# Softmax transposed through DRAM in the first and third attention, and the NF4 comparisons moved to GpSimd

## The chip, the core and the metric

The program runs on one core of one Trainium2 chip. A core has TensorE for matrix products, which writes to PSUM; VectorE, ScalarE and GpSimd for work on vectors; and queues on which transfers between DRAM and the on-chip memory (SBUF) are issued, here nearly all on the queue of SyncE (SP), some of the last stage's on ScalarE's. Each engine works through its own instructions in order and waits for the others at semaphores. The metric is the time of the device for one execution, in microseconds (us).

## The reference

An activation x of 8 batches x 128 tokens x 512 features passes through four blocks; each adds an attention and then a feed-forward layer to x, both on a layernorm of x. All is float32 unless said. In the order of the work:

- first attention: cross-attention to a context of 128 tokens per batch, 32 heads of 128, RMS norm of the queries' input, position bias, mask, softmax, output projection added to its normalised input;
- first feed-forward: a base matrix plus eight low-rank experts, weighted by a sparsemax;
- second attention: 8 small heads over windows of the features; second feed-forward: 8-bit integer weights;
- third attention: 32 query heads on 8 key heads, rotary embedding, mask, softmax;
- third feed-forward: gate, up and down matrices of 1376 x 512, which are first rounded to NF4: each block of 64 weights is divided by its largest magnitude, each quotient replaced by the nearest of 16 code values, and multiplied by the magnitude again;
- fourth attention with RMS norms on queries and keys, and a fourth feed-forward with 64 routed low-rank parts.

What the change touches is computed as:

```python
score = jax.nn.softmax(score, axis=-1)
attn = jnp.einsum('bhqk,bkhd->bqhd', score, h_v)
...
idx = jnp.searchsorted(bounds, normalized)
return (NF4_CODE[idx] * absmax).reshape(shape)
```

## The kernel before

x stays in SBUF. The batches are taken in two halves of four (128 tokens each, so 512 columns).

**The loop of units.** First and third attention are cut into units: one half, one head. A group is four heads, and there are 8 groups per half: 64 units of the first attention (`Unit0`), then 64 of the third (`Unit2`). The loop over `units` is a pipeline. In the turn of unit u, TensorE is given: the transposes of u's softmax (`turn`), the projections of unit u+3 (`pieces`; in the first attention keys and queries, in the third queries, and for head 0 also keys and values), the scores of unit u+2 (`score`), the product of u's softmax with the values (`weigh`), and the work after it (`after`). `after` is, in the first attention, behind head 3 of a group, four times a value projection for the next group and an output projection; in the third attention, two output projections of the previous group behind heads 0 and 1 each. So the scores of a unit are computed two turns before its softmax is used.

`score` evicts the scores from PSUM with VectorE (adding bias or mask), and `softmax` takes the row maximum (VectorE), the exponentials (ScalarE, four instructions) and the reciprocal of the sum; the scaling by it is VectorE's in the first attention and ScalarE's in the third. The result lies with queries on the partitions; the product with the values needs keys there. `turn` calls `p_transposed`: four transposes on TensorE into PSUM (L225), and a copy to SBUF by ScalarE (L228).

In the third attention the rotary embedding of a projection is three VectorE products out of PSUM (L640, L642, L643) and an add on GpSimd (L644).

**Work in between.** Between these pieces the loop calls `slot()`. It does what `short_stages` has put into a table: the first feed-forward, the second attention and the second feed-forward of one half of the batches run while the units of the other half go on. And at a pace per stage (`NF4_PACE`) it advances `nf4_items`, the rounding of the third feed-forward's weights, by steps.

**NF4 rounding.** The code value is built as a sum over 15 thresholds: each adds its step where the quotient is beyond it. In `nf4_round` the first threshold writes `dq` (L708); each of the other 14 is a VectorE TENSOR_SCALAR that compares with the threshold and multiplies by the step into `ind` (L712), and a VectorE add of `ind` to `dq` (L713). There are 34 such chunks, mostly of 128x512, 476 pairs in all. The results are transposed and stored to DRAM (`d1` to `d3`).

**The last stages.** The third feed-forward and the fourth attention follow the loop. The fourth attention's transposes already take a way through DRAM (`L3.far`): VectorE transposes blocks of 32x32 (`V.transpose`, L948), a store writes the tile to DRAM, and four loads read it back with the blocks in their new places.

**What sets the order.** The tile framework that the kernel is written in orders each engine's instructions, DMA issues included, by its own estimate of times, and adds the semaphores. An engine's program may therefore depart from the order of the source: of TensorE's pieces as of SP's issues. Tiles of one tag share a fixed number of buffers, and a tile waits for one to come free: weights go through a ring of 20 tiles of 256 KB (`wpool`, tag `w`), scores through three (`score_tile`, tag `s`, which the fourth attention's `o` shares), transposed softmaxes through two (`pt`).

Of the kernel before, what the change touches and what calls it, by code (L numbers as in the profile page):

```python
# [11 lines left out]
F32 = mybir.dt.float32  # L12
F16 = mybir.dt.float16
BF16 = mybir.dt.bfloat16
# [4 lines left out]
ALU = mybir.AluOpType  # L19
# [4 lines left out]
P = 128  # L24
# [4 lines left out]
HALF = 4  # L29
# [15 lines left out]
NF4_STEPS = []  # L45
# [17 lines left out]
def kernel(ctx: ExitStack, tc: tile.TileContext, a, out):  # L63
    nc = tc.nc
    V, S, G, T = nc.vector, nc.scalar, nc.gpsimd, nc.tensor

    def pool(name, bufs, **kw):
        return ctx.enter_context(tc.tile_pool(name=name, bufs=bufs, **kw))
# [9 lines left out]
    ap_ = pool("att", 2)  # L78
    dram = pool("scratch", 1, space=DRAM)

    class Stream:


        def __init__(self, name, sb, ps, banks):
            self.name, self.sb, self.ps, self.banks = name, sb, ps, banks
# [26 lines left out]
    def load(dst, src):  # L112
        nc.sync.dma_start(dst, src)
# [26 lines left out]
    def batches(hf):  # L140
        return range(hf * HALF, (hf + 1) * HALF)
# [51 lines left out]
    def xt_tile():  # L193
        return xtp.tile([P, DC, 512], F32, tag="xT", name="xT")
# [26 lines left out]
    def p_transposed(st, p, engine=None):  # L221

        tp = st.tp()
        for h in range(4):
            T.transpose(tp[:, h, :], p[:, h, :], ident)  # L225
        pt = st.wide("pt", (P, 4, P))
        if engine is S:
            S.copy(pt, tp)  # L228
        else:
            V.tensor_copy(pt, tp)  # L230
        return pt
# [8 lines left out]
    def tile_of(name, bufs, shape=(P, 512)):  # L240
        return qkv.tile(list(shape), F32, tag=name, name=name, bufs=bufs)
# [2 lines left out]

    class Unit:
        def __init__(self, st, hf, g, h, group):
            self.st, self.hf, self.g, self.h, self.group = st, hf, g, h, group

        def softmax(self, s):
            st = self.st
            nm = st.small(4, "nm")
            V.tensor_reduce(nm, s, AX.X, ALU.max, negate=True)  # L254
            su = st.small(4, "su")
            exps(lambda i: s[:, i, :], lambda i: s[:, i, :], su, 4, nm)
            V.reciprocal(su, su)
            self.p, self.su = s, su
# [5 lines left out]
            return sc  # L264

        def score_tile(self):
            return ap_.tile([P, HALF, P], F32, tag="s", name="s", bufs=3)

        def turn(self):
            self.pt = p_transposed(self.st, self.p, S)  # L270

        def weigh(self):
            pv = self.st.pv()
            for i in range(HALF):
                T.matmul(pv[:, i, :], lhsT=self.values(i), rhs=self.pt[:, i, :], start=True, stop=True)  # L275
            o = tile_of("o", 6, (P, HALF, P))
            S.copy(o, pv)  # L277
            self.group.o.append(o)
# [424 lines left out]

    def nf4_round(dst, w):

        for i, (cmp, bound, step) in enumerate(NF4_STEPS):
            if i == 0:
                V.tensor_scalar(dst, w, bound, step, cmp, ALU.mult)  # L708
                continue
            ind = nfp.tile([P, 512], F32, tag="ind", name="ind", bufs=1)  # L710
            iv = ind[:w.shape[0], :w.shape[1]]
            V.tensor_scalar(iv, w, bound, step, cmp, ALU.mult)  # L712
            V.tensor_add(dst, dst, iv)  # L713
            yield

    def nf4_scales(ri, am):
# [5 lines left out]
    class Rows:  # L722
# [8 lines left out]
        def work(self):  # L731
            n, w = self.n, self.w
            wb = w.rearrange("p (k e) -> p k e", e=64)[:n]
            am = nfp.tile([P, 8], F32, tag="am", name="am")
            V.tensor_reduce(am[:n], wb, AX.X, ALU.max, apply_absolute_value=True)
            ri = nfp.tile([P, 8], F32, tag="ri", name="ri")
            nf4_scales(ri[:n], am[:n])
            yield
            V.tensor_tensor(wb, wb, along(ri[:n], 64), ALU.mult)
            yield  # L740
            dq = nfp.tile([P, 512], F32, tag="dq", name="dq", bufs=1)
            yield from nf4_round(dq[:n], w[:n])
            V.tensor_tensor(wb, dq.rearrange("p (k e) -> p k e", e=64)[:n], along(am[:n], 64), ALU.mult)
            yield
# [41 lines left out]
    class Pairs:  # L786
# [15 lines left out]
        def work(self):  # L802
            w, nw = self.w, self.nw
            self.scale(w, w, pair["rir"])
            yield
            dq = nfp.tile([P, 512], F32, tag="dq", name="dq", bufs=1)
            yield from nf4_round(dq[:, :2 * nw], w[:, :2 * nw])
            self.scale(w, dq, pair["amr"])
            yield
# [77 lines left out]
    class L3:  # L887
# [115 lines left out]
        def weigh(self, it):  # L1003
            pv = self.st.pv()
            for j in range(2):
                T.matmul(pv, lhsT=it.v[:, j, :], rhs=it.pts[j], start=j == 0, stop=j == 1)  # L1006
            it.o = ap_.tile([P, 4, P], F32, tag="s", name="o", bufs=3)
            if it.blocks:
                S.copy(it.o.rearrange("p h (a j) -> p a h j", j=32), pv.rearrange("p a (h j) -> p a h j", j=32))
            else:  # L1010
                S.copy(it.o, pv)
# [68 lines left out]
    with ExitStack() as early:  # L1080
        def sub_pool(name, bufs, **kw):
            return early.enter_context(tc.tile_pool(name=name, bufs=bufs, **kw))
# [3 lines left out]
        nfp = sub_pool("nf4", 2)  # L1086
# [18 lines left out]
        def slot():  # L1105
            for f, args in table.pop(now[0], []):
                f(*args)
            now[0] += 1
            due[0] += 0.0 if turning[0] else NF4_PACE[stage[0]][0 if table else 1]
            with tc.issue_after(mark[0].ins):  # L1110
                while due[0] >= 1.0:
                    due[0] -= 1.0
                    next(items, None)
# [3 lines left out]
        def drain():  # L1117
            while table:
                slot()

        def norm_pieces(i, box, b, get):

            def norm():
                box[b] = layernorm(side, b)

            def turn():
                S.copy(get()[:, :, cols(b)], transposed(side, box[b]))

            put(i, norm)
            put(i + 1, turn)  # L1130

        def l0_half(hf):
            box = {}

            def query(b):
                box[b] = l0_query(side, b)

            now[0] = 0
            for i, b in enumerate(batches(hf)):
                put(4 * i, l0_ctx, side, b)  # L1140
                put(4 * i + 1, query, b)
                put(4 * i + 3, lambda b: l0_turn(side, b, box[b]), b)
# [59 lines left out]
        units = []  # L1202
        for kind in (Unit0, Unit2):
            for hf in range(2):
                for g in range(NG):
                    grp = Group()
                    grp.v = []
                    units += [kind(main, hf, g, h, grp) for h in range(4)]

        xT0 += [xt_tile(), xt_tile()]  # L1210

        V.memset(xT0[1][:, 0, :], 0.0)
# [30 lines left out]
        for u, unit in enumerate(units):  # L1243
            stage[0] = u // (4 * NG)
            turning[0] = 8 * NG - 4 <= u < 8 * NG
            if u == 3:
                l0_half(1)
            if u in (4 * NG - 3, 8 * NG - 3, 12 * NG - 3):
                drain()
            unit.turn()  # L1250
            if u + 3 < len(units):
                for f in units[u + 3].pieces():
                    f()
                    slot()
            if u + 2 < len(units):
                units[u + 2].score()
            unit.weigh()
            if isinstance(unit, Unit2):
                slot()
            unit.after(units, u)  # L1260
            if u in (4 * NG - 1, 8 * NG - 1):
                short_stages((u + 1) // (4 * NG) - 1)
            if u == 12 * NG + 1:
                now[0] = 0
                xT.append(xt_tile())
                for b in batches(0):
                    norm_pieces(2 * b, {}, b, lambda: xT[0])
# [66 lines left out]
    n = len(items)  # L1334
# [96 lines left out]
def build(arrays):  # L1431
    import concourse.bacc as bacc

    nc = bacc.Bacc("TRN2", target_bir_lowering=False, num_devices=1)
    aps = {
        n: nc.dram_tensor(f"in_{n}", v.shape, mybir.dt.from_np(v.dtype), kind="ExternalInput").ap()
        for n, v in arrays.items()
    }
    out = nc.dram_tensor("out_0", (B, P, D), F32, kind="ExternalOutput").ap()
    with tile.TileContext(nc) as tc:  # L1440
        kernel(tc, aps, out)
    return nc
# [9 lines left out]
```

## Time and profile before

The median of three runs is 3138.36 us (3136.59 to 3139.01). The profile is of one execution:

| | |
|---|---|
| time of the profiled execution | 3138.55 us |
| its span, first to last instruction | 3136.8 us |
| mean granted TensorE clock | 0.999 of full speed |
| TensorE busy | 3119.5 us, 99% |
| VectorE busy | 1949.3 us, 62% |
| ScalarE busy | 1154.6 us, 37% |
| GpSimd busy | 292.0 us, 9% |
| first attention's units | about 30 to 1100 us |
| third attention's units | about 1100 to 1900 us |

How the profile is read: a group's row names the source line, the engine, the operation, output<-input tiles, shapes and the count, then the time that the group was busy, the mean of one instruction in ns, the idle time of the engine just before the group's instructions, and what ended it. A timeline's row has the start in us, the duration, the engine, the line, the operation with its tiles and the count of instructions merged into it; in brackets the idle time before it and what ended it. PE is TensorE, DVE VectorE, ACT ScalarE, POOL GpSimd; SPq are the issues on SP's queue, whose duration is that of issuing, not of the transfer. A matmul's recorded duration runs over the start of the next, as matmuls are pipelined; the distance between two starts says what one costs. A line can be that of a helper which several stages use: L225 and L228 also serve the second attention, L218 and L237 several projections.

### The profile page before, as it was taken

Reading aid. Unit: us, or ns where it says so; the run is one execution under the profiler, and the core shown is the slowest. Engines: PE = TensorE matmul, PEld = TensorE weight load, DVE = VectorE, ACT = ScalarE, POOL = GpSimd, SP = SyncE. Lnnn points to the kernel's source line nnn. Section 1 sums busy time; section 2 is a strip of 40 time slices with the busy share of each in tenths; the row PEclk is TensorE's granted clock in tenths of the full one; section 3 lists DMA queues with packets and bytes.
Section 4 is the critical chain, followed back from the end, with each engine's and each line's share of the span. In section 5 each row is a group of like instructions: output and inputs, shape, how many; then the busy total and the mean of one; then the engine's idle time right before and its main releaser. Section 6 shows DMA issues by size and latency. Waiting matters only on the chain.

```text
span 3136.8 us, 34834 instructions
## 1 busy us (share of the span) xinstructions
PE 3119.5 (99%) x11480; PEld 1744.5 (56%) x11480; DVE 1949.3 (62%) x4084; ACT 1154.6 (37%) x3535; POOL 292.0 (9%) x315
## 2 busy tenths in 40 slices
PE   9999999999999999999999999999999999999999
PEld 4555555545555555555556565445666656555554
DVE  5777777656667666887988873122654555555544
ACT  3322333235553233756343343001443434343332
POOL 2000000100001011111111110000111111111110
PEclk9999999999999999999999999999999999999999
DMA  6223222222223321112222212222556555555540
GB/s 210 87 71 91 90 91 80 74 70 75 74 66 89 115 85 55 56 55 71 82 87 73 76 59 59 76 61 93 184 173 183 180 179 174 178 177 164 179 132 14
DMA packets 324802, 328.24 MB, mean 105 GB/s; under 512 B 27600, under 2 KB 238736, under 8 KB 324112
## 3 DMA queue, kind: packets, MB, share of 16 engines
q1 hardware_dynamic: 301200, 283.03, 29.5%
q10 hardware_dynamic: 23040, 41.95, 4.3%
q8 instruction: 92, 1.51, 0.2%
q0 software_dynamic: 384, 1.05, 0.1%
q14 instruction: 86, 0.70, 0.1%
HBM read 259.15 MB, written 66.78 MB: 104 GB/s over the span
## 4 chain that ended last, share of the span: by engine, by line
PE 94%; DVE 4%; DMA 1%; ACT 1%; issue 0%; POOL 0%; SPq 0%; ACTq 0%; POOLq 0%; DVEq 0%
PE mm L237 20%; PE mm L218 14%; PE po L218 7%; PE tp L908 7%; PE mm L363 7%; PE mm L931 7%; PE mm L866 5%; PE pv L1006 4%; PE sc L983 3%; PE sc L263 3%; PE pv L275 3%; PE tp L225 3%; PE mm L875 2%; PE mm L653 2%; PE mm L663 1%; PE sc L519 1%
## 5 line engine op out<-in xcount | busy, mean ns | idle before, releaser
L237 PE MATMUL mm<-xT,w 128*128 128x512 f32 x1024 | 464.1, 595 | 0.2 <-DVE rot L643 0.2
L218 PE MATMUL mm<-w,o 128*128 128x512 f32 x1024 | 460.0, 594 | 0.0
L713 DVE TENSOR_TENSOR dq<-dq,ind 128x512 f32<-128x512 f32 (+2 forms) x476 | 326.2, 685 | 10.5
L218 PEld LDWEIGHTS mm<-w,o 128*128 128x128 f32 x1024 | 188.8, 190 | 217.0 <-issue 207.9
L237 PEld LDWEIGHTS mm<-xT,w 128*128 128x128 f32 x1024 | 188.7, 191 | 208.8 <-issue 202.8
L213 ACT ACTIVATE s<-s,nm 128x128 f32<-128x128 f32 x512 | 199.0, 390 | 149.1 <-DVE nm L254 144.0
L931 PE MATMUL mm<-w,xT 128*128 128x512 f32 x512 | 233.9, 592 | 0.0
L218 PE MATMUL po<-w,o 128*128 128x512 f32 x512 | 233.2, 594 | 0.0
L237 PE MATMUL mm<-ctxT,w 128*128 128x512 f32 x512 | 230.5, 593 | 1.8 <-ACT k L330 1.0
L363 PE MATMUL mm<-w,ctxT 128*128 128x512 f32 x512 | 230.4, 593 | 0.0
L712 DVE TENSOR_SCALAR ind<-nw 128x512 f32<-128x512 f32 (+2 forms) x476 | 218.6, 459 | 5.9
L213 ACT ACTIVATE p<-sc,nm,rq 128x256 f32<-128x256 f32 x256 | 141.1, 562 | 112.3 <-DVE nm L988 108.7
L219 DVE TENSOR_TENSOR x<-x,mm 128x512 f32<-128x512 f32 x128 | 87.5, 684 | 141.3 <-PE mm L218 140.9
L218 PEld LDWEIGHTS po<-w,o 128*128 128x128 f32 x512 | 96.3, 190 | 110.6 <-issue 103.3
L263 PEld LDWEIGHTS sc<-k,q 128*128 128x128 f32 x1024 | 131.0, 191 | 46.0 <-issue 44.4
L159 POOL TENSOR_TENSOR rs<-rs,mhalf 128x1 f32<-128x1 f32 x64 | 39.9, 625 | 1247.5 <-DVE rs L180 743.0
L363 PEld LDWEIGHTS mm<-w,ctxT 128*128 128x128 f32 x512 | 94.3, 190 | 106.2 <-issue 106.2
L866 PE MATMUL mm<-xT,w 128*128 128x512 f32 (+1 forms) x352 | 152.5, 592 | 0.8 <-DVE x L219 0.8
L277 ACT COPY o<-pv 128x512 f32<-128x512 f32 x128 | 74.4, 581 | 204.0 <-PE pv L275 203.9
L987 DVE TENSOR_REDUCE nm<-sc 128x2 f32<-128x512 f32 x128 | 85.3, 674 | 102.3 <-PE sc L983 102.0
L228 ACT COPY pt<-tp 128x512 f32<-128x512 f32 x192 | 108.9, 586 | 107.4 <-PE tp L225 107.3
L931 PEld LDWEIGHTS mm<-w,xT 128*128 128x128 f32 x512 | 97.0, 190 | 89.5 <-issue 84.7
(243 smaller groups left out, 4816.6 us busy)
## 6 DMA issues: line engine op xcount, KB each, us to landing
w<-in_l_wq SPq DMA_DIRECT2D x128, 256.0 KB
w<-in_l_wo SPq DMA_DIRECT2D x128, 256.0 KB
far<-tb SPq DMA_DIRECT2D x60, 512.0 KB
pt<-far SPq DMA_DIRECT2D x240, 128.0 KB
far<-tb SPq DMA_DIRECT2D x63, 384.0 KB
pt<-far SPq DMA_DIRECT2D x252, 96.0 KB
w<-in_l_wk SPq DMA_DIRECT2D x64, 256.0 KB
w<-in_l_wv SPq DMA_DIRECT2D x64, 256.0 KB
```

The costliest lines, as they stand in the source:

```text
L213: S.activation(dst(h), src(h), AF.Exp, bias=negm[:, h:h + 1], scale=by, accum_out=su[:, h:h + 1])
L218: T.matmul(mm, lhsT=o(h), rhs=wo[h], start=h == 0, stop=h == 3)
L228: S.copy(pt, tp)
L237: T.matmul(mm, lhsT=w[:, c, :], rhs=xT[:, c, :], start=c == 0, stop=c == DC - 1)
L263: T.matmul(sc[:, i, :], lhsT=self.q[:, i * P:(i + 1) * P], rhs=k[:, i * P:(i + 1) * P], start=True, stop=True)
L363: T.matmul(mm, lhsT=ctxT[:, c, toks(self.hf * HALF + i)], rhs=grp.wv[c], start=c == 0, stop=c == DC - 1)
L712: V.tensor_scalar(iv, w, bound, step, cmp, ALU.mult)
L713: V.tensor_add(dst, dst, iv)
L866: T.matmul(mm[:n, :], lhsT=w[c][:, j * P:j * P + n], rhs=xT[:, c, :], start=c == 0, stop=c == DC - 1)
L908: T.matmul(it.kv[:, s, :], lhsT=lhsT, rhs=it.wkv[c // 2][:, c % 2, :], start=c == 0, stop=c == DC - 1)
L931: T.matmul(mq, lhsT=self.xT[it.hf][:, c, cols(it.b)], rhs=it.wq[c], start=c == 0, stop=c == DC - 1)
L1006: T.matmul(pv, lhsT=it.v[:, j, :], rhs=it.pts[j], start=j == 0, stop=j == 1)
```

## The change

Two things change. First, all units of the first and third attention but the first three of the loop no longer transpose the softmax on TensorE. A new `turn_far`, called right after the unit's `score`, two turns before the unit is weighed, transposes 32x32 blocks on VectorE into a tile `tb` (one buffer), stores it to DRAM (256 KB), and loads it back into `pt` with four loads of 64 KB. `weigh` takes its operands as slices of that tile. Second, `nf4_round` lets GpSimd compare, writing zeros and ones as bfloat16 into `ind` (now two buffers, since the pool's default holds), one threshold ahead of the sum; VectorE multiplies by the step and adds in one SCALAR_TENSOR_TENSOR. The score tile's tag loses its third buffer and has the pool's default of two.

```diff
     class Unit:
         def __init__(self, st, hf, g, h, group):
             self.st, self.hf, self.g, self.h, self.group = st, hf, g, h, group
+            self.far = True
...
         def score_tile(self):
-            return ap_.tile([P, HALF, P], F32, tag="s", name="s", bufs=3)
+            return ap_.tile([P, HALF, P], F32, tag="s", name="s")

         def turn(self):
-            self.pt = p_transposed(self.st, self.p, S)
+            pt = p_transposed(self.st, self.p, S)
+            self.pt = [pt[:, i, :] for i in range(HALF)]
+
+        def turn_far(self):
+            tb = tile_of("tb", 1, (P, 4, HALF, 32))
+            V.transpose(tb, self.p.rearrange("p i (c k) -> p c i k", k=32))
+            far = dram.tile([4, 32, 4, P], F32, tag="far0", name="far0", bufs=4)
+            load(far.rearrange("a k b n -> (a k) (b n)"), tb.rearrange("p c i j -> p (c i j)"))
+            pt = self.st.wide("pt", (P, 4, HALF, 32))
+            for b in range(4):
+                load(pt[32 * b:32 * b + 32].rearrange("p a i j -> p a (i j)"), far[:, :, b, :].rearrange("a k n -> k a n"))
+            self.pt = [pt[:, :, i, :] for i in range(HALF)]

         def weigh(self):
             pv = self.st.pv()
             for i in range(HALF):
-                T.matmul(pv[:, i, :], lhsT=self.values(i), rhs=self.pt[:, i, :], start=True, stop=True)
+                T.matmul(pv[:, i, :], lhsT=self.values(i), rhs=self.pt[i], start=True, stop=True)
...
     def nf4_round(dst, w):
-        for i, (cmp, bound, step) in enumerate(NF4_STEPS):
-            if i == 0:
-                V.tensor_scalar(dst, w, bound, step, cmp, ALU.mult)
-                continue
-            ind = nfp.tile([P, 512], F32, tag="ind", name="ind", bufs=1)
-            iv = ind[:w.shape[0], :w.shape[1]]
-            V.tensor_scalar(iv, w, bound, step, cmp, ALU.mult)
-            V.tensor_add(dst, dst, iv)
+        def above(i):
+            cmp, bound, _ = NF4_STEPS[i]
+            ind = nfp.tile([P, 512], BF16, tag="ind", name="ind")[:w.shape[0], :w.shape[1]]
+            G.tensor_scalar(ind, w, bound, None, cmp)
+            return ind
+
+        then = above(1)
+        cmp, bound, step = NF4_STEPS[0]
+        V.tensor_scalar(dst, w, bound, step, cmp, ALU.mult)
+        for i in range(1, len(NF4_STEPS)):
+            ind = then
+            if i + 1 < len(NF4_STEPS):
+                then = above(i + 1)
+            V.scalar_tensor_tensor(dst, ind, NF4_STEPS[i][2], dst, ALU.mult, ALU.add)
             yield
...
+        for unit in units[:3]:
+            unit.far = False
...
-            unit.turn()
+            if not unit.far:
+                unit.turn()
...
             if u + 2 < len(units):
                 units[u + 2].score()
+                if units[u + 2].far:
+                    units[u + 2].turn_far()
             unit.weigh()
```

(The fourth attention's `o` loses `bufs=3` in the same way.)

More of the change, by code (lines that the diff above doesn't have):

```diff
@@ L1006, in weigh @@
                 T.matmul(pv, lhsT=it.v[:, j, :], rhs=it.pts[j], start=j == 0, stop=j == 1)
-            it.o = ap_.tile([P, 4, P], F32, tag="s", name="o", bufs=3)
+            it.o = ap_.tile([P, 4, P], F32, tag="s", name="o")
             if it.blocks:
```

## The prediction

> **What bounds the kernel now.** I read the page's busy times first, then who keeps TensorE waiting, then the timeline of the first and third attention, where the change works.
>
> ```profile
> span 3136.8 us, 34834 instructions
> PE 3119.5 (99%) x11480; PEld 1744.5 (56%) x11480; DVE 1949.3 (62%) x4084; ACT 1154.6 (37%) x3535; POOL 292.0 (9%) x315
> L225 PE MATMUL tp<-ident,s 128*128 128x128 f32 x768 | 112.2, 274 | 1.2 <-DVE s L521 0.6 <-ACT s L681 0.4
> ```
>
> TensorE is busy for 3119.5 of 3136.8 us, and its transposes of the softmax (L225) waited 1.2 us in all. In the waits of TensorE between 120 and 1890 us, which hold both attentions, no entry is above 0.9 us. So the time is the sum of TensorE's work, and every other engine runs inside it. "Busy" could hide slack, so the price of an instruction comes from the distance between starts (third attention, TensorE's timeline):
>
> ```profile
> 1668.87 1.06 PE L275 MATMUL pv<-pt,v 128*128 128x128 f32 x8
> 1669.76 0.60 PE L225 MATMUL tp<-ident,s 128*128 128x128 f32 x4
> 1670.20 3.60 PE L237 MATMUL mm<-xT,w 128*128 128x512 f32 x8
> 1673.63 1.05 PE L263 MATMUL sc<-k,q 128*128 128x128 f32 x8
> 1674.53 1.06 PE L275 MATMUL pv<-pt,v 128*128 128x128 f32 x8
> ```
>
> Four transposes hold TensorE for 1670.20 - 1669.76 = 0.44 us (not 0.60, the last drains under the next matmul), a projection for 3.43, scores 0.89, weighing 0.89. The granted clock is full throughout, so no change of clock is in the sum.
>
> **The change part by part.**
>
> Removed from TensorE: 128 units less the first 3, each 0.43 to 0.44 us: 125 x 0.43 = 54 us. Nothing else gets shorter on the engine that sets the end. From the profiled execution, whose time is 3138.55 us (span 3136.8 and 1.75 around it), that leaves 3084.6; from the median of 3138.36 it leaves 3084.4. This is the floor.
>
> Removed from ScalarE: 125 copies at 586 ns (L228), 73 us. It waited for TensorE anyway, so nothing for the end.
>
> VectorE: each of 476 thresholds loses its TENSOR_SCALAR and keeps one two-input instruction.
>
> ```profile
> L713 DVE TENSOR_TENSOR dq<-dq,ind 128x512 f32<-128x512 f32 (+2 forms) x476 | 326.2, 685 | 10.5
> L712 DVE TENSOR_SCALAR ind<-nw 128x512 f32<-128x512 f32 (+2 forms) x476 | 218.6, 459 | 5.9
> ```
>
> The new step-and-sum should cost what L713 does (the SCALAR_TENSOR_TENSOR of L678 takes 688 ns at 128x512): 219 us go. It gains 125 block transposes of 128x512. The rows are 960 ns for 128x768 and 1238 for 128x1024 (L948), 1.09 ns per element, so about 0.68 us each, 85 us. Without blocking, VectorE does 134 us less.
>
> GpSimd: 476 comparisons, a form that the trace does not have. Bounds: TENSOR_TENSOR of 128x128 takes 458 ns and of 128x512 1268 (fixed part 188 ns); the one operation with one input read, the AFFINE_SELECT of 128x128, takes 291, so 0.8 ns per element and 0.60 us at 512. Above stands the two-input 1.27. The Trainium skill (GPSIMD Engine Reference, 3.1 Elementwise) gives 769 ns for 512 elements as the best of an arithmetic-bound loop: with the 188 of dispatch 0.96 us. A comparison reads one input, so I take 0.65, next to the select row, and keep 0.6 to 1.27.
>
> The rule that speaks against this part: the Trainium skill (SBUF, Who interferes with whom) says that a VectorE instruction with two inputs in SBUF, or one in a two-port mode, and a GpSimd instruction that reads SBUF exclude each other for the whole instruction. The trace agrees:
>
> ```profile
> 1670.44 1.27 POOL L644 TENSOR_TENSOR q<-q,rot 128x512 f32<-128x512 f32 x1 [11.26 <-PE tp L225]
> 1670.91 1.09 DVE L712 TENSOR_SCALAR ind<-nw 128x512 f32<-128x512 f32 x1
> 1671.92 0.67 DVE L254 TENSOR_REDUCE nm<-s 128x4 f32<-128x512 f32 x1
> ```
>
> The TENSOR_SCALAR, 0.43 us elsewhere, lasts 1.09, until just after GpSimd's add ends at 1671.71. So a comparison and a step-and-sum never overlap; a threshold costs VectorE 0.69 us if its comparison falls beside reductions, PSUM reads or waits, and 0.69 + 0.65 = 1.34 if it blocks VectorE fully, against 1.14 before. Half blocked, 1.02: a small relief, not the 219 us of a count without the rule. A comparison may run two thresholds ahead of the sum (two buffers), so after a pause both are ready.
>
> The detour of the softmax through DRAM: 1 store and 4 loads per unit on SP's queue, 625 more issues. The third stage's first detour runs unhindered in the trace (SP's and ScalarE's timelines):
>
> ```profile
> 2182.81 0.33 SPq L113 DMA_DIRECT2D far<-tb  x1
> 2185.12 1.76 SPq L113 DMA_DIRECT2D pt<-far  x4
> ```
> ```profile
> 2188.74 0.62 ACT L963 COPY qT<-pt 128x512 f32<-128x512 f32 x1 [0.35 <-DMA pt<-far]
> ```
>
> Store issued to store landed 2.31 us, four load issues 1.76, last landing 1.86 more: 5.93 us from issue to use, for 384 KB; ours has 256. A busier one, whose store is issued at 2758.73 and whose weighing waited until 2766.05, took 7.3.
>
> Is it in time? **First attention, heads 2 and 3 of a group:** from the end of the scores to the weighing TensorE does weighing 0.89, two projections 6.87, scores 0.89, weighing 0.89, two projections 6.87 and scores 0.89: 17.3 us. Around 322 us in the trace the softmax needs 6.2 (322.1 to 328.3) with three thresholds inside; built, four step-and-sums stand in it. Counted through: eviction 0.69, sum 0.69, blocked 0.65, mask 0.69, sum 0.69, reduction 0.68, exponentials with two sums and a comparison beside them 2.0, small ones 0.33, blocked 0.65, scaling 0.69, transpose 0.68, together 8.5. With 5.93 that is 14.4: spare 2.9 us, 1.8 at 0.96 a comparison, 0.9 at 1.27. Heads 0 and 1 have the output projections (27 us) besides. **Third attention, head 0:** before, 11.3 us lay between its scores and its weighing (0.89 + 0.44 + 3.43 + 0.89 + 0.89 + 0.44 + 3.43 + 0.89), too few for softmax and detour, but in the built order six of the eight matmuls of an output projection pair now stand ahead of its weighing: 0.89 + 3.43 + 0.89 + 0.89 + 3.43 + 0.89 + 0.44 + 5.15 = 16.0 us. The softmax took 6.9 there (1668.9 to 1675.8); the transpose then queues behind the next unit's three rotation products, in places also its eviction and a sum (1 to 3 us), and the detour adds 5.93: 14.5 to 16.5. Spare between 1.5 and -0.5. Head 3 has 17.3 and about 15.8 of need.
>
> Queues: on SP a store waits for VectorE with weight loads behind it. The weight ring is 20 tiles, over one group ahead, so a few us are covered there; the exception is the fourth value-weight tile of a group in the first attention, which is issued behind head 0's store and needed 2.6 us into the value projections: 0 to 1 us late. Dequantisation stores stand between head 0's store and its loads in the third attention and wait for ScalarE's copy: up to 1.2 us. On GpSimd the rotation's add and the inverse square roots stand behind at most one running comparison (0.65); the add must be done before the scores, and in the third attention has about 0.7 us to spare, so 0 to 0.5 us on two units a group. Dropping the third score buffer costs nothing: the transpose empties it early.
>
> Sum: head 0 of the third attention 0.5 x 16 = 8, rotation 0.2 x 32 = 6 (the lower half of its range, since VectorE is a little freer), first attention's weight tile 0.2 x 16 = 3: 17 us of new waiting, taken at 14 because L1's matmuls widen the windows in the first half of the third attention. 3084.4 + 14 = 3098 us, with 3083 to 3118 as this case's own range (no waits at all, to twice 17).
>
> **The rivals.** *The detour is late in every short window.* If it takes 7.3 us, and SP's waits add half a us, head 0 and head 3 of the third attention (32 units) stall by 1.5 us each and heads of the first by little: 48 us, and the gain is gone: 3132, from 3115 to 3150. For it: the 7.3 above; against: it came with 55% DMA load and twice the bytes, here the load is 25%. *The shared port becomes the bound (slower).* Place: first half of the first attention, 163 thresholds in the 400 us from 200 to 600, about 26 per group of 64.7 us. Per group the port is held 26 x (0.69 + comparison) plus 8 us of masks and scalings; what VectorE does besides without the port (evictions, reductions, output sums, transposes) is some 12 us, in order and half overlapped at best. This passes TensorE's 63 us at a comparison of about 1.1 us. At 1.27 with 0.3 us lost at each handover it is 26 x 2.26 + 14 = 73 us, 10 over: 80 us for its eight groups, and about 40 more where VectorE is at 85% in the third attention: 3205. For it: the port row; against: the select row, by which the comparison is half as long. *The change doesn't do what it says* is excluded: the built order has the transposes gone from 125 units.
>
> **How the numbers follow.** Covered detour 0.56 (3098); late detour 0.20 (3132), of which 0.09 ends faster, 0.08 within and 0.03 above the bound; port 0.24 (3205), all slower. 0.2%, 6.3 us, is about what a measurement of this kernel can tell from no change. Faster 0.65, same 0.08, slower 0.27. The range leaves out half of the port's chance: 3082 to 3165.
>
> **What would show it.** L225 falls from 768 to 268, TensorE's busy time by about 54 us. Right: comparisons near 0.65 us, step-and-sums with a median of 0.69 and a tail to 1.4, waits of weighing (L288) for the loads of pt under 20 us, of scores for GpSimd under 10. Wrong: comparisons over 1.1 us, waits of TensorE for VectorE's score eviction or softmax, or for w loads held up behind a store; each us of such waiting is a us of the end.

## The result: slower by 1.7%

The changed kernel takes 3190.15 us (median of four runs, 3184.48 to 3193.67), against 3137.48 us (four runs, 3136.35 to 3139.01) for the kernel before. The ratio is 1.0166, 95% interval 1.0148 to 1.0183. The forecast was 3098 us, and the time lies 25 us above the upper end of its range.

The page of the changed kernel, and from its groups of instructions the transposes, GpSimd's comparisons (L723), the step-and-sums (L733) and the block transposes (L277):

```profile
span 3187.2 us, 35257 instructions
PE 3097.5 (97%) x10976; PEld 1702.6 (53%) x10980; DVE 1882.5 (59%) x3733; ACT 1084.0 (34%) x3410; POOL 1097.3 (34%) x791
```
```profile
L225 PE MATMUL tp<-ident,s 128*128 128x128 f32 x268 | 35.4, 274 | 1.6 <-DVE s L367 1.0 <-DVE s L534 0.6
L723 POOL TENSOR_SCALAR ind<-nw 128x512 bf16<-128x512 f32 (+2 forms) x476 | 809.5, 1702 | 543.4 <-DVE dq L733 232.3
L733 DVE SCALAR_TENSOR_TENSOR dq<-ind,dq 128x512 f32<-128x512 bf16 (+2 forms) x476 | 364.1, 765 | 219.5 <-POOL ind L723 215.2
L277 DVE STREAM_TRANSPOSE tb<-s 128x512 f32<-128x512 f32 x125 | 88.5, 708 | 20.2 <-ACT s L694 18.1
```

The 500 transposes are gone (768 to 268). But TensorE, idle for 17.3 us of the span before (3136.8 - 3119.5), is now idle for 89.7, and its busy time fell by 22.0 us only. A comparison takes 1702 ns on average over its three shapes (1766 at 128x512) where the forecast had 650, and VectorE stands 215.2 us before results of comparisons, a wait that did not exist. Who keeps TensorE waiting now (total, times, longest):

```profile
PE mm L237 <- DVE rot L656: 21.7, 7, 5.1
PE mm L218 <- DVE x L219: 9.0, 3, 4.9
PE mm L237 <- DVE x L219: 8.8, 6, 3.0
PE pv L288 <- DMA pt<-far: 8.3, 4, 4.0
```

Three of the four name VectorE: the rotary products and the output sums, which have to empty a PSUM bank before the next product may fill it. What makes VectorE late stands in its timeline (start, duration, idle before and who ended it), here in the output projections of the first attention:

```profile
457.26 0.69 DVE L733 SCALAR_TENSOR_TENSOR dq<-ind,dq 128x512 f32<-128x512 bf16 x1 [1.38 <-POOL ind L723]
459.34 0.69 DVE L733 SCALAR_TENSOR_TENSOR dq<-ind,dq 128x512 f32<-128x512 bf16 x1 [1.38 <-POOL ind L723]
459.95 0.68 DVE L219 TENSOR_TENSOR x<-x,mm 128x512 f32<-128x512 f32 x1
461.41 0.69 DVE L733 SCALAR_TENSOR_TENSOR dq<-ind,dq 128x512 f32<-128x512 bf16 x1 [0.79 <-POOL ind L723]
```

A threshold takes 2.07 us: 0.69 for the sum, 1.38 of standing still. Before, the pair on VectorE took 1.18 us there, from one start of L712 to the next:

```profile
454.22 0.42 DVE L712 TENSOR_SCALAR ind<-nw 128x512 f32<-128x512 f32 x1
454.67 0.69 DVE L713 TENSOR_TENSOR dq<-dq,ind 128x512 f32<-128x512 f32 x1
455.40 0.43 DVE L712 TENSOR_SCALAR ind<-nw 128x512 f32<-128x512 f32 x1
```

An output sum (L219) that becomes ready during the standing is done only after the next step-and-sum, because the engine works in order.

The loss lies where the comparisons are dense. Here is the first half of the first attention, 100 to 620 us, before and after; a row gives the stretch and its length, then the busy time (and number of instructions) of TensorE, of its weight loads, of VectorE, ScalarE and GpSimd, then the granted clock of TensorE and what the DMA did:

```profile
100.00:620.00 520.00, 520.00 (x1782) 276.31 (x1781) 387.22 (x805) 156.39 (x446) 13.30 (x12) 1.00 0.28 86
```
```profile
100.00:620.00 520.00, 489.75 (x1514) 247.84 (x1513) 329.73 (x562) 121.19 (x364) 396.31 (x220) 0.98 0.36 110
```

The other such stretch is 1500 to 1950 us, where TensorE is busy for 417.35 of 450 us at clock 0.97 after, against 447.38 at 1.00 before. From the third feed-forward on nothing changed: the last 1237 us hold 1230.3 us of TensorE before and 1229.9 after.

### The profile page after: what moved, and what is told of

Read it like the earlier page. It is cut to its first block, busy times and chain, and to the rows that moved or that the text cites. A ratio compares the mean times of both kernels' runs of the same rounds, so it can differ in the third digit from the quotient of the medians.

```text
span 3187.2 us, 35257 instructions
## 1 busy us (share of the span) xinstructions
PE 3097.5 (97%) x10976; PEld 1702.6 (53%) x10980; DVE 1882.5 (59%) x3733; ACT 1084.0 (34%) x3410; POOL 1097.3 (34%) x791
## 4 chain that ended last, share of the span: by engine, by line
PE 65%; DVE 10%; POOL 5%; ACT 2%; issue 2%; DMA 1%; SPq 0%; DVEq 0%; ACTq 0%; POOLq 0%
PE mm L237 9%; PE mm L218 8%; PE po L218 7%; PE tp L928 7%; PE mm L951 7%; PE mm L886 5%; POOL ind L723 4%; PE pv L1026 3%; PE sc L1003 3%; PE mm L376 3%; PE mm L895 2%; PE pv L288 2%; ACT s L213 1%; PE sc L265 1%; DVE dq L733 1%
## 5 line engine op out<-in xcount | busy, mean ns | idle before, releaser
L723 POOL TENSOR_SCALAR ind<-nw 128x512 bf16<-128x512 f32 (+2 forms) x476 | 809.5, 1702 | 543.4 <-DVE dq L733 232.3
L237 PE MATMUL mm<-xT,w 128*128 128x512 f32 x1024 | 479.4, 611 | 30.6 <-DVE rot L656 21.7
L733 DVE SCALAR_TENSOR_TENSOR dq<-ind,dq 128x512 f32<-128x512 bf16 (+2 forms) x476 | 364.1, 765 | 219.5 <-POOL ind L723 215.2
L159 POOL TENSOR_TENSOR rk<-rk,mhalf 128x2 f32<-128x2 f32 x64 | 44.7, 699 | 530.9 <-DVE rk L940 491.0
L657 POOL TENSOR_TENSOR q<-q,rot 128x512 f32<-128x512 f32 x64 | 84.4, 1318 | 262.3 <-DVE rot L656 239.3
L237 PEld LDWEIGHTS mm<-ctxT,w 128*128 128x128 f32 x512 | 94.6, 193 | 103.3 <-issue 98.1
L288 PE MATMUL pv<-pt,v 128*128 128x128 f32 x1024 | 138.3, 279 | 11.0 <-DMA pt<-far 8.3
```

Source lines behind the costliest of these rows:

```text
L237: T.matmul(mm, lhsT=w[:, c, :], rhs=xT[:, c, :], start=c == 0, stop=c == DC - 1)
L288: T.matmul(pv[:, i, :], lhsT=self.values(i), rhs=self.pt[i], start=True, stop=True)
L723: G.tensor_scalar(ind, w, bound, None, cmp)
L733: V.scalar_tensor_tensor(dst, ind, NF4_STEPS[i][2], dst, ALU.mult, ALU.add)
```

## The experiments

Two theories to begin with. *Theory 1:* the comparison is too long; it alternates with VectorE's sum, VectorE comes late to PSUM, TensorE waits. *Theory 2:* the detour through DRAM is late.

### Each half of the change alone

The detour with the thresholds on VectorE as before:

```diff
-            G.tensor_scalar(ind, w, bound, None, cmp)
...
-            V.scalar_tensor_tensor(dst, ind, NF4_STEPS[i][2], dst, ALU.mult, ALU.add)
+            V.tensor_scalar(iv, w, bound, step, cmp, ALU.mult)
+            V.tensor_add(dst, dst, iv)
```

> The detour through DRAM as in the changed kernel, the dequantisation's thresholds all on VectorE as before. Theory 1 (GpSimd's comparison is too long, alternates with VectorE's sum over the shared port and makes VectorE late for TensorE): without GpSimd the gain of the removed transposes comes in, 3084 us plus at most the 17 us of waits of the prediction, 3085 to 3110. Theory 2 (the detour is late, its store or its loads keep the weighing waiting): the time stays near the changed kernel's, 3170 us or more.

The comparisons on GpSimd, transposes on TensorE (and the third score buffer back, which the cut leaves out):

```diff
-        for unit in units[:3]:
+        for unit in units:
             unit.far = False
```

> The thresholds' comparisons on GpSimd as in the changed kernel, all transposes of the softmax on TensorE as before, three score buffers. Theory 1: TensorE has its 54 us of transposes again and VectorE is still late, though less, since TensorE gives it 0.44 us more per unit and the 125 block transposes of 0.71 us are gone: 3200 to 3245 us. Theory 2: no detour, no wait, 3137 to 3145 us.

The detour alone took 3104.55 us (ratio 0.9893, 0.9876 to 0.9909), GpSimd's comparisons alone 3219.27 (1.0260, 1.0243 to 1.0277). Theory 2 falls. The page of the detour alone, and the one entry of its TensorE waits that names the detour:

```profile
span 3105.2 us, 34847 instructions
PE 3074.3 (99%) x10980; PEld 1695.7 (55%) x10980; DVE 2016.5 (65%) x4209; ACT 1087.5 (35%) x3410; POOL 295.7 (10%) x315
```
```profile
PE pv L288 <- DMA pt<-far: 1.0, 2, 0.8
```

TensorE is idle for 30.9 us, 13.6 more than before, and waits 1.0 us for loads of the detour. The 8.3 us in the changed kernel have another origin, as the longest of the four shows (3.97 us, at 495.29): that unit's scores began at 472.52, but VectorE, standing before comparisons, came to the block transpose only at 488.10, and the store and the loads came after it. So the detour gains 33 us, the comparisons lose 81 to 86 whichever way the transposes go (3190.15 - 3104.55, 3219.27 - 3137.79), with two score buffers in the first pair and three in the second. The detour alone is better than both kernels.

### How the time depends on the comparison's length

The cut is that of the first of three runs; the step-and-sum reads the quarter four times.

```diff
-            G.tensor_scalar(ind, w, bound, None, cmp)
-            return ind
+            G.tensor_scalar(ind, w[:, :w.shape[1] // 4], bound, None, cmp)
+            return times(ind, 4)
```

> The changed kernel with each comparison over a quarter of the columns, and the step-and-sum reading that quarter four times (left out: three quarters of the comparisons, so the weights of the third stage are wrong). By the shortest comparisons of 192 columns (0.69 us) and the 1.38 us of VectorE's waits for 512, one of 128 columns takes about 0.55 us, near the 0.65 us of the prediction. Theory 1: a threshold takes 0.55 + 0.69 = 1.24 us instead of 2.07, VectorE is in time, 3085 to 3110 us. Theory 2: the detour is the same, 3170 us or more.

> The same with half of the columns, read twice (left out: half of the comparisons). One comparison takes about 0.83 us, a threshold 1.52 us. Theory 1: by the port count of the prediction's second rival, 26 x 1.52 + 14 = 54 us per group against TensorE's 61: still inside, 3090 to 3125 us. Theory 2: 3170 us or more.

> The changed kernel with each comparison over three quarters of the columns, into two fixed indicator tiles whose last quarter stays zero (left out: a quarter of the comparisons). One comparison takes about 1.1 us, a threshold 1.8 us. This is the point from which the prediction's second rival let the shared port decide: 26 x 1.8 + 14 = 61 us per group, as much as TensorE has. If that count holds, the time stands just at the knee, 3105 to 3135 us; if the loss grows in proportion to the comparison's length from the half on (3103 at 0.83 us, 3190 at 1.38), it is 3140 to 3155.

Of each run the group of full-height comparisons (mean; the undisturbed length is in the table):

```profile
L723 POOL TENSOR_SCALAR ind<-nw 128x128 bf16<-128x128 f32 x420 | 262.5, 625 | 844.3 <-DVE dq L734 517.4 <-issue 244.2 <-DVE nw L760 30.9
```
```profile
L723 POOL TENSOR_SCALAR ind<-nw 128x256 bf16<-128x256 f32 x420 | 397.6, 947 | 733.0 <-DVE dq L734 420.2 <-issue 237.7 <-DVE nw L760 29.5
```
```profile
L727 POOL TENSOR_SCALAR ind<-nw 128x384 bf16<-128x384 f32 x420 | 596.6, 1422 | 581.2 <-DVE dq L737 273.7 <-issue 225.3 <-DVE nw L763 29.0
```

| columns compared | undisturbed comparison (shortest single ones in the timeline) | time |
|---|---|---|
| 128 | 0.53 us | 3098.95 us |
| 256 | 0.85 us | 3102.82 us |
| 384 | 1.17 us | 3120.87 us |
| 512 (the change) | 1.49 us | 3190.15 us |

The comparison is 0.21 us plus 2.50 ns per column, on a straight line through all four. The end does not follow it on a line: 4 us for the first 0.32 us, 18 for the second, 69 for the third. That is a knee: the loss sets in between 0.85 and 1.17 us, and most of it comes beyond. From 100 to 620 us, VectorE's waits for comparisons are 9.1, 16.5, 93.4 and 151.0 us in the order of the table, and its own waits for TensorE, the slack that it has left, fall from 113.1 over 94.7 and 35.4 to 12.5. The forecast's comparison of 0.65 us lies between the first two rows, 3099 to 3103 us, and the forecast said 3098.

### Rate or look-ahead

```diff
-            ind = nfp.tile([P, 512], BF16, tag="ind", name="ind")[...]
+            ind = nfp.tile([P, 512], BF16, tag="ind", name="ind", bufs=3)[...]
...
-        then = above(1)
+        ahead = [above(i) for i in range(1, 3)]
```

> The changed kernel with three ind buffers and comparisons two thresholds ahead of the sum instead of one. Theory 1a (what counts is the rate: comparison 1.38 and sum 0.69 exclude each other, 2.07 us per threshold, whatever the look-ahead): no more than a few us gained, 3175 to 3193. Theory 1b (what counts is the short look-ahead: after a pause VectorE finds one or two results ready and then stands in order before each further one): each pause now gives a third ready result, and the time falls to 3110 to 3160.

3174.64 us (1.0112, 1.0095 to 1.0129): 15.5 us better, 0.4 us beyond the range of 1a and far from 1b. One more result can be ready after a pause; within a burst the sums still start 2.07 us apart. So the short look-ahead is not what costs most: it is that comparison and sum alternate. Whether by the lock or by the waiting, the next runs ask.

### Lock or waiting

The comparison does two things to VectorE: while it reads, VectorE's two-input instructions are shut out (the port row of the prediction), and its result is waited for. First the waiting without the reading:

```diff
-            G.tensor_scalar(ind, w, bound, None, cmp)
+            for _ in range(4):
+                G.memset(ind, 1.0)
```

> The changed kernel with each comparison replaced by four MEMSETs of the same indicator tile (left out: the comparisons, so the weights of the third stage are wrong). At 0.53 us each, from the rows of 204 ns for 128 and 951 ns for 1024 columns, that is 2.1 us per threshold, the distance between sums that the changed kernel shows in bursts, but nothing on GpSimd reads SBUF while VectorE works. Theory 1c (VectorE loses its time by standing in order before a result that comes every 2.07 us): 3175 to 3200 us as with the comparisons. Theory 1d (the loss is that GpSimd's read locks VectorE's two-input instructions out, so masks, scalings and sums are stretched): without the lock 3130 us or less.

It took 3120.13 us (0.9941, 0.9924 to 0.9957). Its groups:

```profile
L724 POOL MEMSET ind<- 128x512 bf16 x1680 | 837.9, 529 | 444.6 <-DVE dq L734 404.1 <-DVE rx L587 3.4
L734 DVE SCALAR_TENSOR_TENSOR dq<-ind,dq 128x512 f32<-128x512 bf16 (+2 forms) x476 | 335.7, 705 | 186.3 <-POOL ind L724 178.9
```

GpSimd is no less busy than in the change (4 x 529 ns is 2.12 us per threshold), VectorE still stands 178.9 us before its results, yet 70 us of the 86 are gone, and the step-and-sum is back at 705 ns. Theory 1c (the waiting alone) falls. The opposite, reading without waiting (`none` is a tile of zeros):

```diff
-            V.scalar_tensor_tensor(dst, ind, NF4_STEPS[i][2], dst, ALU.mult, ALU.add)
+            V.scalar_tensor_tensor(dst, none, NF4_STEPS[i][2], dst, ALU.mult, ALU.add)
```

> The changed kernel with all comparisons on GpSimd, but each step-and-sum reads a tile of zeros that was written once at the start, so no sum waits for a comparison (left out: what the comparisons say, so the weights of the third stage are wrong). The counterpart of the write-only run: there the waiting was kept and the lock taken away, here the lock is kept and the waiting taken away. If the lock alone does the harm (Theory 1d), VectorE's two-input instructions are still shut out for 1.49 us at a time and the time stays at 3150 us or more. If lock and waiting are needed together (a comparison that is stretched by VectorE's own work makes the next sum late, and VectorE stands in order before it), it falls to 3100 to 3130.

3207.68 us (1.0222, 1.0205 to 1.0239), which looked like proof for the lock, until its TensorE waits were read:

```profile
PE sc L267 <- POOL q L659: 45.9, 7, 10.3
PE mm L220 <- DVE x L221: 26.1, 2, 13.9
```

The scores wait up to 10.3 us for the rotary add on GpSimd. With nothing to hold them back, a chunk's comparisons are queued ahead of it: before the add that starts at 1584.90 us, ten of them run for 16.19 us on end. The run had exchanged one wait for another and tells nothing of the lock. So the pace was put back, still without the waiting, on top of the last edit: VectorE writes the bound into a one-column tile `go`, and the comparison has to wait for it (`ind`, which no sum reads, has one buffer here):

```diff
         def above(i):
-            ind = nfp.tile([P, 512], BF16, tag="ind", name="ind")[...]
+            go = nfp.tile([P, 1], F32, tag="go", name="go", bufs=14)[...]
+            V.memset(go, bound)
+            ind = nfp.tile([P, 512], BF16, tag="ind", name="ind", bufs=1)[...]
-            G.tensor_scalar(ind, w, bound, None, cmp)
+            G.tensor_scalar(ind, w, go, None, cmp)
```

> In the run where nobody reads the comparisons, GpSimd's queue ran ahead: the rotation's add stood behind up to a whole chunk of comparisons (TensorE waited 45.9 us for it), so that run says nothing clean on the lock. Here the pace of the changed kernel is restored: VectorE writes a one-column tile with the bound after each sum, and the comparison of two thresholds later reads it; the sums still read zeros (left out: what the comparisons say, so the weights of the third stage are wrong). So comparisons come at the same places with the same length, the lock is the same, and VectorE only never waits for a result before the end of a chunk. If the lock alone does the harm: 3165 to 3200 us. If it takes the waiting in order on top: 3100 to 3135, about as much below the changed kernel as the write-only run (3120).

3117.58 us (0.9933, 0.9915 to 0.9950), with comparisons as long as in the change and step-and-sums that are stretched most of all:

```profile
L727 POOL TENSOR_SCALAR ind<-nw,go 128x512 bf16<-128x512 f32 x420 | 741.6, 1766 | 453.3 <-DVE go L725 254.3 <-issue 124.6 <-DVE nw L823 21.9
L736 DVE SCALAR_TENSOR_TENSOR dq<-none,dq 128x512 f32<-128x512 bf16 (+2 forms) x476 | 390.4, 820 | 4.9
```

Theory 1d (the lock alone) falls too. Against 3104.55 for the detour alone (whose VectorE makes the comparisons itself), the lock by itself costs 13 us, the waiting by itself 16 us, both together 86. They do more than add. The reading that fits is that one feeds the other: VectorE's two-input work makes a comparison late (1.49 us undisturbed, 1766 ns on average at full size), and VectorE, in order, then stands before the late result. This last step is argued, not shown: that both merely draw on the same slack, which neither uses up alone, would also lose more than the sum, and no run separates the two. VectorE's budget in the stretch from 100 to 620 us shows it (busy by the windows; the two waits by its chain of waits; "slack" is its waiting for TensorE at L219 and at the score eviction):

| 100 to 620 us | VectorE busy | waits for ind | slack | time of the kernel |
|---|---|---|---|---|
| before | 387.2 | none | 42.2 + 54.3 = 96.5 | 3137 |
| the change | 329.7 | 151.0 | 6.7 + 5.8 = 12.5 | 3190 |
| detour alone | 414.4 | none | 41.5 + 29.9 = 71.4 | 3105 |
| writing only, with waiting | 339.2 | 125.3 | 19.9 + 4.1 = 24.0 | 3120 |
| reading, without waiting (paced) | 365.6 | 18.2, at the ends of chunks | 54.7 + 27.1 = 81.8 | 3118 |

"VectorE 59% busy" on the page of the changed kernel hides that in this stretch busy plus standing for comparisons is 480.7 of 520 us (329.7 + 151.0). The detour alone has the busiest VectorE of the five and the shortest time. The lines for the change and for before:

```profile
DVE dq L733 <- POOL ind L723: 151.0, 142, 1.4
DVE x L219 <- PE mm L218: 6.7, 8, 1.1
DVE s L363 <- PE sc L265: 5.8, 3, 3.4
```
```profile
DVE s L350 <- PE sc L263: 54.3, 31, 2.7
DVE x L219 <- PE mm L218: 42.2, 27, 2.1
```

### What a wait of TensorE costs

The span of the change is 82.0 us longer than that of the detour alone, for the same matmuls. 58.8 us of it are idle time of TensorE (89.7 - 30.9); 23.2 are busy time (3097.5 - 3074.3). Why the same work takes longer, TensorE's weight loads and matmuls show around one late output sum in the changed kernel:

```profile
596.01 0.19 PEld L376 LDWEIGHTS mm<-w,ctxT 128*128 128x128 f32 x1 [0.24 <-issue]
600.40 0.50 PEld L218 LDWEIGHTS mm<-w,o 128*128 128x128 f32 x2 [4.21 <-DVE x L219]
601.42 0.34 PEld L218 LDWEIGHTS mm<-w,o 128*128 128x128 f32 x1 [0.52 <-issue]
602.27 0.34 PEld L218 LDWEIGHTS mm<-w,o 128*128 128x128 f32 x1 [0.52 <-issue]
603.13 0.27 PEld L218 LDWEIGHTS mm<-w,o 128*128 128x128 f32 x1 [0.52 <-issue]
603.64 0.19 PEld L218 LDWEIGHTS mm<-w,o 128*128 128x128 f32 x1 [0.24 <-issue]
```
```profile
600.40 5.11 PE L218 MATMUL mm<-w,o 128*128 128x512 f32 x8 [3.38 <-DVE x L219]
605.35 3.60 PE L237 MATMUL mm<-ctxT,w 128*128 128x512 f32 x8
```

After 4.21 us without a load, loads come 0.86 us apart instead of 0.43 for some 3 us, and eight matmuls take 5.11 us instead of 3.60. The granted clock is 0.50 from 600.40 to 602.00 us and 1.00 again from 603.60. Over the whole span its mean is 0.991, against 0.998 with the detour alone; times the spans (3187.2 and 3105.2), an estimate of the clock's loss is 28.7 - 6.2 = 22.5 us, about the 23.2 of busy time. To measure it by itself, TensorE was made to wait once per group in the detour-alone version, for two lengths:

```diff
+        def pause(n):
+            d = main.mm()
+            T.matmul(d[:, :P], lhsT=ident, rhs=ident, start=True, stop=True)
+            S.copy(zz, d[:, :P])
+            for _ in range(n):
+                G.tensor_tensor(zz, zz, ident, ALU.mult)
+            T.matmul(main.mm()[:, :P], lhsT=zz, rhs=ident, start=True, stop=True)
```

> The version with the detour alone (3104.5 us), and once per group of four units, 32 times, TensorE is made to wait for a short chain: one 128x128 matmul, ScalarE copies its result, GpSimd multiplies it twice (0.46 us each), one more matmul reads it. By the rows of before that is a wait of about 0.9 + 0.9 = 1.8 us: 32 x 1.8 = 58 us at most, less where the pause takes the place of a wait, 3145 to 3170 us. Only the difference to the next run is of interest.

> The same with six multiplications by GpSimd, 4 x 0.46 = 1.83 us more of waiting at each of the 32 places, about 3.7 us in all. If a wait costs its own length whatever it is, this run is 32 x 1.83 = 59 us above the run with two. If a wait of over some 2.4 us also halves the granted clock for the next 3.6 us, as the projections of 5.40 us instead of 3.60 after such waits in the changed kernel suggest, each place costs 1.8 us more and the run is about 116 us above it, with a granted clock of 0.98 or less in the first and third attention.

Two multiplications gave 3176.21 us, six 3275.95: 99.7 us between them, 3.12 per place, where the added multiplications account for 4 x 0.458 = 1.83 (58.6 in all). The rest, 41 us or 1.3 per place, is busy time: TensorE's rose from 3106.3 to 3148.4 us for identical matmuls, and the mean granted clock fell from 0.996 to 0.982. The two timelines at the same place of the program, short pause and long pause:

```profile
335.58 0.49 PE L1223 MATMUL mm<-ident,zz 128*128 128x128 f32 x2 [1.15 <-POOL zz L1222]
335.90 3.60 PE L237 MATMUL mm<-ctxT,w 128*128 128x512 f32 x8
```
```profile
355.98 0.79 PE L1223 MATMUL mm<-ident,zz 128*128 128x128 f32 x2 [4.01 <-POOL zz L1222]
356.57 5.01 PE L237 MATMUL mm<-ctxT,w 128*128 128x512 f32 x8
```

This wait of 1.15 us costs itself; the one of 4.01 us also costs 1.41 us in the next eight matmuls. But a wait need not be that long. In the run with six multiplications:

```profile
723.61 0.49 PE L1223 MATMUL mm<-ident,zz 128*128 128x128 f32 x2 [2.37 <-POOL zz L1222]
723.93 5.29 PE L237 MATMUL mm<-ctxT,w 128*128 128x512 f32 x8
```

The granted clock of the 8 us behind each of the 32 places gives a count. With six multiplications, all 18 waits of 2.37 to 4.01 us are followed by a loss, of 1.4 to 2.9 us, and so are 10 of the 14 shorter ones. With two, the one wait of 3.24 us is, and 3 of the 31 up to 1.70 us; the six of 1.15 or 1.16 us are not. What decides among the shorter ones is open.

The 99.7 us lie between the two expectations (59 and 116 us), nearer to the second. The Trainium skill (TensorE: Matmul & The Clock Gate, Part 1) has the array at half clock after an idle window of about 3.4 us, until about 3.4 us of work have passed. The runs agree with the half, and with the second number as far as half of the losses are 1.7 us, which is 3.4 us at half clock; they do not agree with the first, since waits of 2.37 us are enough here.

### A small share for GpSimd

```diff
+            if i in (4, 8, 12):
+                V.scalar_tensor_tensor(dst, then, step, dst, ALU.mult, ALU.add)
+                if i < 12:
+                    then = above(i + 4)
```

> The detour, and only the thresholds 4, 8 and 12 of a chunk compared on GpSimd, each begun as soon as the one before it is used, so that up to three of VectorE's own thresholds lie between; the other eleven on VectorE as before. VectorE is relieved of 102 x 0.44 = 45 us, GpSimd's 102 x 1.49 = 152 us lock it in small doses. Against the detour alone at 3104.5 us: by the half-width run, whose comparisons take about as much of GpSimd per threshold, no worse, 3098 to 3106; if the stretching of VectorE's instructions outweighs the relief, 3107 to 3120.

3108.14 us (0.9906, 0.9889 to 0.9922), 3.6 us above the detour alone, with intervals that overlap: no gain from it, and not a clear loss. The 45 us of relief bought nothing that TensorE could use. The fastest version with the whole computation remains the detour alone, 3104.55 us, 33 us below the kernel before.

## Why the prediction was wrong

**The step that failed** is the price of GpSimd's comparison: "A comparison reads one input, so I take 0.65, next to the select row, and keep 0.6 to 1.27." Undisturbed it is 1.49 us, above the upper bound. Two rows lay at hand, and the nearer one was taken only as the upper bound, by an argument from the number of inputs: the add of 128x512, an arithmetic instruction on a full float tile, stood at 1.27 us. The comparison, with one input fewer and half the output bytes, is slower still: 2.50 ns per column. The estimate of 0.96 us built from 769 ns on a page of the Trainium skill (GPSIMD Engine Reference, 3.1 Elementwise) was too low as well. The bounds had been set by the same argument, so the range inherited the error.

**What would have followed from 1.49** was in the text. The second rival put "about 26 per group" times (sum plus comparison) plus 14 us for what cannot run beside it, against TensorE's 63 us. With the measured 2.07 us that is 26 x 2.07 + 14 = 68 us. Measured, from the score eviction of one group's second unit to that of the next, over six groups from 165 to 574 us: 68.1 us on average (66.6 to 70.9), against 64.7 before and 63.0 with the detour alone. The size is right; that it agrees to the last digit is luck, since 166 sums lie in that stretch, 27.7 per group, with which the same sum gives 71. The point from which it decides, "about 1.1 us", is by its own numbers (63 - 14) / 26 - 0.69 = 1.2 us; the loss sets in between 0.85 and 1.17. Its own time, 3205, assumed 2.26 us per threshold; 3190 goes with 2.07.

**The mechanism of that rival was only half named.** It spoke of the port as the thing that is full. The paced run has the same comparisons on the same port and loses 13 us. What fills VectorE's time in the change is standing in order before results, 151.0 us of the 520; the runs show that it takes port and waiting together. The sentence "A comparison may run two thresholds ahead of the sum (two buffers), so after a pause both are ready." was true for two thresholds and false for the rest of a burst; the two-ahead run shows that one step more moves this by 15.5 us and no more.

**What held.** TensorE was the bound, and removing 500 transposes is worth about what was worked out once nothing takes it back: with comparisons of 128 columns TensorE's busy time falls by 51.1 us (3119.5 - 3068.4; forecast 54), its idle time grows by 11.4 (forecast 14), and the time is 3099. **The second agreement is luck.** In that run no listed wait of TensorE names the loads of the detour, the rotary add or a weight tile, the three places from which the 14 us were summed. Its idle time is made of other waits, the longest, 3.4 us in all, for rows of the rotary table. The detour alone, at 3105, has 45.2 us less busy time and 13.6 more idle, of which 1.0 us is for the loads; why its busy time falls less is open. The block transpose took 708 ns (0.68 forecast) and the step-and-sum 0.69 undisturbed. The late-detour rival is refuted: 1.0 us of waiting for its loads when VectorE is in time, 8.3 when it is not, under the 20 that were named as the bound.

**What was missing.** That "no change of clock is in the sum" was read from a profile in which TensorE never waits. Once it does, for some 2.4 us or more, the clock adds its own loss: about 22 of the 82 us by which the change stands above the detour alone, by the granted clock, and 23 by the busy time.

## What to carry to other kernels

Price an instruction on another engine by the nearest row of the same kind, not by counting its inputs, and let the range reach beyond that row when no instruction of that form has been measured. Before moving half of a dependent pair to a second engine, add up the receiving engine's busy time and its waiting for the partner in the stretch concerned, in order: an engine that is 59% busy over the span can have next to no slack where it counts. And where two halves of a change are independent, cost each alone; here one gained 33 us and the other lost 86.

## What the runs showed of the hardware

- GpSimd's comparison with a constant, float to bfloat16, takes 0.21 us plus 2.50 ns per column (0.53, 0.85, 1.17, 1.49 us at 128, 256, 384, 512), more than the add of two tiles (1.27 us at 512).
- A write-only MEMSET on GpSimd (529 ns at 512 columns) leaves VectorE's step-and-sums nearly alone (705 ns on average; 765 beside the waited-for comparisons, 820 beside the paced ones; the add in their place takes 687 with the detour alone). This is as the Trainium skill (SBUF — State Buffer, Who interferes with whom) has it: a VectorE instruction with two SBUF inputs contends with a GpSimd instruction that reads SBUF, not with one that only writes it.
- The lock without the waiting costs 13 us, the in-order waiting without the lock 16, both together 86, each against the detour alone.
- After all 18 pauses of TensorE of 2.37 to 4.01 us in the run with six multiplications its granted clock fell, and 1.4 to 2.9 us were lost in the next 8; after the six of 1.15 or 1.16 us in the run with two nothing was. Over all 32 places of the longer run it came to 1.3 us each.
